# The scan stage of a four-layer kernel: another layout of channels and states on the partitions, transfers in program order, another order of merges, and the gate at PSUM

## The chip, the cores and the metric

The kernel runs on one core of one Trainium2 chip. The metric is device time in microseconds (us) for one execution of the whole program. TensorE, VectorE, ScalarE and GpSimd (POOL) compute, the SP queue issues nearly all transfers, and 16 DMA engines carry them out.

## The reference

Four layers follow each other on four images of 128 channels and 64x64 pixels, all in float32: a spatial attention, two pairs of shift convolution and adder convolution, a gated attention with a small network, and a state-space (Mamba) layer that scans the 4,096 pixels of an image in both directions. The change lies in the last layer alone. What its scan computes, for 256 channels d, 16 states n and 4,096 steps l of each image:

```python
def _selective_scan(u, delta, A, Bm, Cm, Dv, z):
    dA = jnp.exp(jnp.einsum('bdl,dn->lbdn', delta, A))
    dBu = jnp.einsum('bdl,bnl,bdl->lbdn', delta, Bm, u)
    ...
    h = a * h + bu          # at each step, from h0 = 0
    ...
    y = jnp.einsum('lbdn,bnl->bdl', hs, Cm) + Dv[None, :, None] * u
    return y * _silu(z)
...
y = y_f + flip(y_b)         # forward scan, and the scan of the reversed sequence
mamba_out = jnp.einsum('bdl,od->blo', y, out_proj_w)
x_processed = _layer_norm(mamba_out, ln_w, ln_b)
return f_mamba + gamma * f_low
```

## The kernel before

The first three layers and the preparation of the fourth (`layer3_prepare`) leave in DRAM, for each image, the step sizes `delta_d`, the products of step size and input `du_d`, the convolved input `xs_d`, the gate `sz_d` (256 rows of 4,096 each), the rows B and C in `xdbl_d` (16 each), and the low part `low_d`. The function `layer3_scan` does the rest, and only it is changed.

**Tiles.** One tile is 8 channels with their 16 states: 128 partitions, 4,096 steps. There are 4 images x 2 halves of the channels x 16 = 128 tiles. In the kernel before, partition p holds state p // 8 of channel p % 8. Each tile is worked in two halves of 2,048 steps (`h`). For each half a load brings 8 rows of `delta_d` (`dl`) and one brings 8 rows of `du_d` (`du`), each repeated for the 16 states (L933, 1,024 KB each); per image and half there is one load of B and one of C (L924, 1,024 KB), each row repeated for the 8 channels.

**Pieces.** A tile's scan is cut into 8 pieces of 1,024 steps, four forward and four backward, in the order of line 911. For each piece (L944 to L960) ScalarE computes the decay `da` into PSUM (L953) and VectorE scans (L955), each piece starting from the last value of the one before. POOL has made the scan's other input before that, `dbu = du * B` (L941). A piece of each direction covers the same pixels, so TensorE adds the two directions by multiplying both by the identity into one PSUM bank of 512 steps (`merge`, L970), ScalarE copies the bank to SBUF (L979), POOL multiplies 2,048 steps by C (L983), and TensorE sums the 16 states of each channel into 32 rows of the tile `y` (L992). After four tiles `y` holds 32 channels: ScalarE copies it (L1002) and a transfer stores it to `y_d` as 4 blocks of 32 rows by 512 steps (L1004).

**Finish.** For each 512 steps of an image, `finish` loads `y_d`, `xs_d` and `sz_d` (L1014), adds the skip term `2 * D * xs` (L1016, L1017), multiplies by the gate on VectorE (L1018), and does the output projection (L1022), the layer norm (L1024 to L1032) and the sum with `low_d` (L1030, L1033). It runs for one image beside the scan of the next, and for the last image after everything else.

**Order.** A loop over tiles `n` and pieces `e` (L1041 to L1071) writes the operations of several tiles between each other: pieces of tile n, merges of tile n - 1, products by C and sums of tiles n - 1 and n - 2, inputs of tile n + 1. A scheduler then orders the instructions of each engine by their dependencies and by when buffers come free; only what is put in `keep_in_program_order` stays where it is written. In the kernel before, no transfer of the scan stage is: SP issues `dl`, `du` and the loads of `finish` where the scheduler put them. Buffers: `dl` 3, `du` 2, `dbu` 3, `h` 6, `m` 2, B and C 3 each, `y` one for each half.

Of the kernel before, what the change touches and what calls it, by code (L numbers as in the profile page):

```python
# [16 lines left out]
P = 128  # L17
# [821 lines left out]
def layer3_scan(  # L839
# [9 lines left out]
    with ExitStack() as ctx:  # L849
        cp = ctx.enter_context(tc.tile_pool(name="l4c", bufs=1))  # L850
        bc = ctx.enter_context(tc.tile_pool(name="l4bc", bufs=3))
# [6 lines left out]

        of8 = cp.tile([P, ND], F32, name="of8")
        nc.vector.tensor_reduce(of8, cm.ident.rearrange("p (n d) -> p d n", d=ND), AX.X, ALU.add)  # L860
# [5 lines left out]
        for j in range(4):  # L866
            nc.vector.tensor_copy(rows_of[:, j, ND * j : ND * (j + 1)], of8)

        a = []
        for name, src in (("af", a_log), ("ab", ab_log)):  # L870
# [5 lines left out]
            for c in range(2):  # L876
                spread = sb.tile([P, D_STATE, ND], F32, tag="spread", name=f"{name}_s{c}")
                nc.vector.tensor_tensor(
                    spread,
                    t[:, c, :].unsqueeze(2).broadcast_to([P, D_STATE, ND]),  # L880
                    of8.unsqueeze(1).broadcast_to([P, D_STATE, ND]),
                    ALU.mult,
                )
                pa = ps_m.tile([P, P // ND], F32, tag="mg", name=f"{name}_p{c}")
                nc.tensor.matmul(pa, spread.rearrange("p n d -> p (n d)"), group, start=True, stop=True)
                nc.vector.tensor_copy(at[:, c, :], pa)
            a.append(at)

        d2 = cp.tile([P, 2], F32, name="d2")
        nc.sync.dma_start(d2, d_param)  # L890

        nc.vector.tensor_scalar(d2, d2, 2.0, None, ALU.mult)
        skip = cp.tile([P, 2, P], F32, name="skip")
        for c in range(2):
            nc.vector.tensor_scalar(skip[:, c, :], cm.ident, d2[:, c : c + 1], None, ALU.mult)
# [20 lines left out]
        def by_states(b, h):  # L916

            if (b, h) not in by_image:
                got = []
                for what in range(2):  # L920
                    t = bc.tile([P, HL], F32, tag="BC"[what], name=f"{'BC'[what]}{b}_{h}")
                    r = DT_RANK + D_STATE * what
                    src = xdbl_d[b, r : r + D_STATE, halves[h]]
                    nc.sync.dma_start(t, src.unsqueeze(1).broadcast_to([D_STATE, ND, HL]))  # L924
                    got.append(t)
                by_image[b, h] = got
            return by_image[b, h]

        def by_channels(src, n, h, tag, bufs):
# [3 lines left out]
            nc.sync.dma_start(t, rows8.unsqueeze(0).broadcast_to([D_STATE, ND, HL]))  # L933
            return t

        def inputs(n, h):

            b = tiles[n][0]
            du = by_channels(du_d, n, h, "du", 2)
            t = big.tile([P, HL], F32, tag="dbu", bufs=3, name=f"dbu{n}_{h}")  # L940
            nc.gpsimd.tensor_tensor(t, du, by_states(b, h)[0], ALU.mult)  # L941
# [20 lines left out]
        def block_of(e):  # L962
            return (1, e) if e < 4 else (0, e - 4)
# [11 lines left out]
        def copied(n, e):  # L975
            h, k = block_of(e)
            if k == 0:
                st[n, "m", h] = big.tile([P, HL], F32, tag="m", bufs=2, name=f"m{n}_{h}")
            nc.scalar.copy(st[n, "m", h][:, bass.ts(k, BK)], st.pop((n, "mg", e)))  # L979

        def times_c(n, h):
            m = st[n, "m", h]
            nc.gpsimd.tensor_tensor(m, m, by_states(tiles[n][0], h)[1], ALU.mult)  # L983

        def sums(n, h):

            j = tiles[n][2] % 4
# [3 lines left out]
            for g in range(4):  # L991
                nc.tensor.matmul(  # L992
                    st["y", h][32 * g : 32 * g + 32, :], rows_of[:, j, :], m[:, bass.ts(g, BK)],
                    start=(j == 0), stop=(j == 3), skip_group_check=True,
                )

        def evacuate(n, h):
            b, c, i = tiles[n]
            if i % 4 < 3:
                return  # L1000
            t = sb.tile([P, BK], F32, tag="ye", name=f"ye{n}_{h}")
            nc.scalar.copy(t, st.pop(("y", h)))  # L1002
            r = 8 * (i - 3)
            nc.sync.dma_start(y_d[b, c, r : r + 32, halves[h]].rearrange("r (g w) -> g r w", g=4), t)  # L1004

        def finish(b, k):
# [3 lines left out]
            gated = []  # L1010
            for c in range(2):
                yx = sb.tile([P, 3, BK], F32, tag="yx", name=f"yx{v}_{c}")
# [199 lines left out]
```

## Time and profile before

| What | Value |
|---|---|
| median of three runs | 23,432.48 us (23,413.33 to 23,440.21) |
| the profiled execution: time, span | 23,406.72 us, 23,404.9 us |
| first issue of a load of the scan stage (`dl`) | 20,072.2 us |
| first and last scan of L955 begin | 20,088.3 us, 23,291.9 us |
| scans: those that take a value over, and those that start a direction | 768 at 2,349 ns, 256 at 2,290 ns |
| decays of L953 | 1,024 at 1,118 ns |
| copies of L979 | 1,024 at 581 ns |

The page gives the span in 40 equal slices of 585 us; a digit is the busy share of an engine in tenths. The row DMA is the mean busy share of the 16 DMA engines, and GB/s what they moved. A group row gives line, engine and operation, the tiles and shapes, the count, busy us and mean ns of one, and the idle time before it with what ended it. The waits give who waited for whom, the us in total, how many times, and the longest. A table of stretches gives for each stretch of time the busy us of the engines, the granted TensorE clock, the DMA share and the GB/s.

### The profile page before, as it was taken

How to read it: one execution, taken by the hardware profiler on the slowest of the kernel's cores; microseconds unless marked ns; L12 is line 12 of the kernel's file. 1: busy time of each engine (PE TensorE's matmuls, PEld its weight loads, DVE VectorE, ACT ScalarE, POOL GpSimd, SP SyncE). 2: the span in 40 equal slices, each digit the busy share in tenths (PEclk: the TensorE clock that was granted, in tenths of full speed). 3: DMA queues.
4: the chain of work that ended last, by engine and by line, in shares of the span. 5: the costliest groups of instructions: out<-in, count | busy, mean ns of one | idle time of the engine just before them, and what ended most of it. 6: DMA issues, size and time to landing. Idle time of an engine off the chain costs nothing. (4 is left out here: it accounts for less than half of the span.)

```text
span 23404.9 us, 347773 instructions
## 1 busy us (share of the span) xinstructions
PE 21561.9 (92%) x146624; PEld 7793.4 (33%) x146624; DVE 20131.0 (86%) x15018; ACT 19315.0 (83%) x13440; POOL 3763.5 (16%) x1710
## 2 busy tenths in 40 slices
PE   9999999999999999999999999999997557677777
PEld 4443333333333333433333333333333222222222
DVE  7887999999999999989999999999997765777776
ACT  5666999999999999989999999999997224555554
POOL 5662000000000000000000000000000000577776
PEclk9999999999999999999999999999998776899999
DMA  0000000000000000000000000000000002788886
GB/s 13 11 5 12 1 3 7 1 3 5 3 3 1 3 1 3 2 11 3 5 3 1 3 7 1 3 1 3 3 1 32 0 0 99 186 197 190 192 192 170
DMA packets 174502, 809.06 MB, mean 35 GB/s; under 512 B 22716, under 2 KB 23364, under 8 KB 102788
## 3 DMA queue, kind: packets, MB, share of 16 engines
q1 hardware_dynamic: 172356, 778.42, 13.2%
q8 instruction: 1146, 18.78, 0.3%
q10 hardware_dynamic: 576, 8.39, 0.1%
q14 instruction: 424, 3.47, 0.0%
HBM read 658.15 MB, written 128.58 MB: 34 GB/s over the span
## 5 line engine op out<-in xcount | busy, mean ns | idle before, releaser
L396 ACT ACTIVATE a1a<-a1pb,a1wn 128x2048 f32<-128x2048 f32 x4096 | 7792.7, 1995 | 198.7 <-PE a1pa L342 102.0
L396 ACT ACTIVATE a2a<-a2pb,a2wn 128x2048 f32<-128x2048 f32 x4096 | 7791.3, 1996 | 136.8 <-PE a2pa L342 94.8
L407 DVE TENSOR_SCALAR a2d<-a2pb,a2wa 128x2048 f32<-128x2048 f32 x4096 | 4993.8, 1282 | 212.8 <-PE a2pa L342 212.5
L407 DVE TENSOR_SCALAR a1d<-a1pb,a1wa 128x2048 f32<-128x2048 f32 x4096 | 4993.2, 1282 | 207.1 <-PE a1pa L342 206.6
L342 PE MATMUL a2pa<-a2a,a2pick 128*32 128x512 f32 x32768 | 4576.2, 593 | 31.4 <-ACT a2a L396 31.4
L342 PE MATMUL a1pa<-a1a,a1pick 128*32 128x512 f32 x32768 | 4570.0, 593 | 31.3 <-ACT a1a L396 31.3
L342 PE MATMUL a2pa<-a2d,a2pick 128*32 128x512 f32 x32768 | 4436.8, 594 | 46.6 <-DVE a2d L407 46.4
L342 PE MATMUL a1pa<-a1d,a1pick 128*32 128x512 f32 x32768 | 4434.7, 594 | 47.1 <-DVE a1d L407 47.0
L425 DVE SCALAR_TENSOR_TENSOR a1a<-a1pb,a1wa,a1a 128x2048 f32<-128x2048 f32 x1024 | 2406.5, 2350 | 322.5 <-ACT a1a L396 322.5
L425 DVE SCALAR_TENSOR_TENSOR a2a<-a2pb,a2wa,a2a 128x2048 f32<-128x2048 f32 x1024 | 2406.3, 2350 | 314.0 <-ACT a2a L396 314.0
L342 PEld LDWEIGHTS a2pa<-a2a,a2pick 128*32 128x32 f32 x32768 | 1490.7, 110 | 2368.2 <-issue 2045.2
L342 PEld LDWEIGHTS a1pa<-a1a,a1pick 128*32 128x32 f32 x32768 | 1487.4, 110 | 2370.3 <-issue 2030.4
L970 PE MATMUL mg<-h,ident 128*128 128x512 f32 x4096 | 1998.7, 639 | 258.1 <-ACT m L979 211.0
L342 PEld LDWEIGHTS a2pa<-a2d,a2pick 128*32 128x32 f32 x32768 | 1348.3, 109 | 2470.9 <-issue 1921.1
L342 PEld LDWEIGHTS a1pa<-a1d,a1pick 128*32 128x32 f32 x32768 | 1345.1, 109 | 2472.3 <-issue 1902.8
L955 DVE TENSOR_TENSOR_SCAN h<-da,h,dbu 128x1024 f32<-128x1024 f32 x768 | 1804.3, 2349 | 86.2 <-POOL dbu L941 4.4
L970 PEld LDWEIGHTS mg<-h,ident 128*128 128x128 f32 x4096 | 796.8, 203 | 1503.9 <-issue 881.1
L190 POOL TENSOR_TENSOR ssum<-ssum,et 128x512 f32<-128x512 f32 x960 | 1228.9, 1280 | 233.5 <-ACT et L185 166.8
L983 POOL TENSOR_TENSOR m<-m,C 128x2048 f32<-128x2048 f32 x256 | 1157.0, 4519 | 641.7 <-DVE h L955 335.4
L941 POOL TENSOR_TENSOR dbu<-du,B 128x2048 f32<-128x2048 f32 x256 | 1153.3, 4528 | 24.5 <-DMA du<-du_d 19.4
L155 ACT COPY et<-pe 128x512 f32<-128x512 f32 x1024 | 595.5, 582 | 592.1 <-PE pe L153 575.8
L153 PE MATMUL pe<-q,k 128*128 128x512 f32 x2048 | 1051.1, 596 | 8.7 <-DVE mx L163 8.1
(265 smaller groups left out, 13276.7 us busy)
## 6 DMA issues: line engine op xcount, KB each, us to landing
dl<-delta_d SPq DMA_DIRECT2D x256, 1024.0 KB
du<-du_d SPq DMA_DIRECT2D x256, 1024.0 KB
xs_d<-xs SPq DMA_DIRECT2D x8, 2048.0 KB
sz_d<-sz SPq DMA_DIRECT2D x64, 256.0 KB
delta_d<-dv SPq DMA_DIRECT2D x32, 512.0 KB
du_d<-du SPq DMA_DIRECT2D x32, 512.0 KB
y_d<-ye SPq DMA_DIRECT2D x64, 256.0 KB
yx<-xs_d SPq DMA_DIRECT2D x64, 256.0 KB
```

What stands on the lines that cost most here:

```text
L153: nc.tensor.matmul(pe, k[:, bass.ts(j, P)], unit[u, "q"], start=True, stop=True)
L155: nc.scalar.copy(et, pe)
L190: nc.gpsimd.tensor_tensor(unit[u, "sum"], unit[u, "sum"], at, ALU.add)
L342: nc.tensor.matmul(pa[s][32 * g : 32 * g + 32, :], pick[v][:, 31 - jj : 63 - jj], d[:, bass.ts(s, BK)], start=False, stop=False, skip_grou ...
L396: nc.scalar.activation(rows(at), view(t), AF.Abs, bias=wn[t][:, co : co + 1], scale=0.5 if g == q else 1.0,)
L407: nc.vector.tensor_scalar(rows(dt), view(t), wa[:, t, co : co + 1], None, ALU.max)
L425: nc.vector.scalar_tensor_tensor(at, view(MAX_TAP), wa[:, MAX_TAP, co : co + 1], at, ALU.max, ALU.add)
L941: nc.gpsimd.tensor_tensor(t, du, by_states(b, h)[0], ALU.mult)
L955: nc.vector.tensor_tensor_scan(t[:, cols][:, s], da[:, s], st[n, "dbu", h][:, cols][:, s], 0.0 if e % 4 == 0 else st["last"], ALU.mult, AL ...
L970: nc.tensor.matmul(pm, cm.ident, st[n, way, h][:, bass.ts(k, BK)], start=(way == 0), stop=(way == 1))
L983: nc.gpsimd.tensor_tensor(m, m, by_states(tiles[n][0], h)[1], ALU.mult)
```

## The change

- **Layout.** Partition p now holds state p % 16 of channel p // 16. The loads of `dl` and `du` read 8 rows, each 16 times in a row; those of B and C read the 16 rows, 8 times over. The small constant matrices follow (`of16`, `of8`, `spread`).
- **Transfers** of the stage go through `moved`, which pins them in program order on SP. B and C have two buffers each in place of three. `du` is asked for up to two tiles ahead.
- **Merges.** The order of `block_of` changes: a tile's first two merges (`e` of 6 and 7) are written beside the tile's own last backward pieces, the other six beside the next tile. `m` has three buffers.
- **Gate at PSUM.** `xs_d` and `sz_d` are loaded beside the sums of four tiles, as 4 blocks of 32 rows (`blocks_of`); the skip term is four more matmuls into `y` (L1025 of the changed kernel), and VectorE multiplies `y` by the gate straight out of PSUM. What is stored to `y_d` is the gated result. `finish` then loads `y_d` and `low_d` alone.
- **Finish** is a generator that goes one step every second piece; `lb` and `lw` are applied on ScalarE, the product with the scale of the norm on POOL.

The core of the diff:

```diff
-        bc = ctx.enter_context(tc.tile_pool(name="l4bc", bufs=3))
+        bc = ctx.enter_context(tc.tile_pool(name="l4bc", bufs=2))
...
+        def moved(out, src):
+            tc.keep_in_program_order(nc.sync.dma_start(out, src))
...
-                    nc.sync.dma_start(t, src.unsqueeze(1).broadcast_to([D_STATE, ND, HL]))
+                moved(t, src.unsqueeze(0).broadcast_to([ND, D_STATE, HL]))
...
             rows8 = src[b, c, ND * i : ND * (i + 1), halves[h]]
-            nc.sync.dma_start(t, rows8.unsqueeze(0).broadcast_to([D_STATE, ND, HL]))
+            moved(t, rows8.unsqueeze(1).broadcast_to([ND, D_STATE, HL]))
...
         def block_of(e):
-            return (1, e) if e < 4 else (0, e - 4)
+            return (0, e - 2) if 2 <= e < 6 else (1, e - 6 if e > 5 else e + 2)
...
-                st[n, "m", h] = big.tile([P, HL], F32, tag="m", bufs=2, name=f"m{n}_{h}")
+                st[n, "m", h] = big.tile([P, HL], F32, tag="m", bufs=3, name=f"m{n}_{h}")
...
+        def blocks_of(t, n, h):
+            b, c, i = tiles[n]
+            r = 32 * (i // 4)
+            return t[b, c, r : r + 32, halves[h]].rearrange("r (g w) -> g r w", g=4)
+
+        def beside_sums(n, h):
+            if tiles[n][2] % 4 == 0:
+                for name, src in (("xs", xs_d), ("sz", sz_d)):
+                    t = sb.tile([P, BK], F32, tag=name, bufs=2, name=f"{name}4_{n}_{h}")
+                    moved(t, blocks_of(src, n, h))
+                    st[name, h] = t
...
-                    start=(j == 0), stop=(j == 3), skip_group_check=True,
+                    start=(j == 0), stop=False, skip_group_check=True,
                 )
-        def evacuate(n, h):
-            ...
-            nc.scalar.copy(t, st.pop(("y", h)))
-            r = 8 * (i - 3)
-            nc.sync.dma_start(y_d[b, c, r : r + 32, halves[h]].rearrange("r (g w) -> g r w", g=4), t)
+            if j == 3:
+                for g in range(4):
+                    rows32 = slice(32 * g, 32 * g + 32)
+                    nc.tensor.matmul(
+                        st["y", h][rows32, :], skip[rows32, c, q, :], st["xs", h][rows32, :],
+                        start=False, stop=True, skip_group_check=True, tile_position=(32 * g, 32 * g),
+                    )
+        def gate(n, h):
+            if tiles[n][2] % 4 == 3:
+                t = st.pop(("sz", h))
+                nc.vector.tensor_tensor(t, st.pop(("y", h)), t, ALU.mult)
+                st["gated", h] = t
+        def store(n, h):
+            if tiles[n][2] % 4 == 3:
+                moved(blocks_of(y_d, n, h), st.pop(("gated", h)))
...
         def finish(b, k):
...
-                yx = sb.tile([P, 3, BK], F32, tag="yx", name=f"yx{v}_{c}")
-                for q, src in enumerate((y_d, xs_d, sz_d)):
-                    nc.sync.dma_start(yx[:, q, :], src[b, c, :, ck])
-                py = ps_m.tile([P, BK], F32, tag="mg", name=f"py{v}_{c}")
-                nc.tensor.matmul(py, cm.ident, yx[:, 0, :], start=True, stop=False)
-                nc.tensor.matmul(py, skip[:, c, :], yx[:, 1, :], start=False, stop=True)
-                nc.vector.tensor_tensor(yx[:, 0, :], py, yx[:, 2, :], ALU.mult)
+                moved(gated[:, c, :], y_d[b, c, :, ck])
+            moved(fl, low_d[b, :, ck])
+            yield
...
+            nc.scalar.activation(fl, fl, AF.Identity, bias=lb)
...
+            nc.scalar.activation(mo, po, AF.Identity, scale=lw)
             nc.scalar.activation(sq, po, AF.Square)
...
-            nc.vector.scalar_tensor_tensor(rs, po, lw, rs, ALU.mult, ALU.mult)
-            nc.gpsimd.tensor_scalar(rs, rs, lb, None, ALU.add)
-            nc.gpsimd.tensor_tensor(fl, rs, fl, ALU.add)
-            nc.sync.dma_start(out[b, :, ck], fl)
+            nc.gpsimd.tensor_tensor(mo, mo, rs, ALU.mult)
+            yield
+            nc.gpsimd.tensor_tensor(fl, mo, fl, ALU.add)
...
+            moved(out[b, :, ck], fl)
...
+                k = n if e > 5 else n - 1
+                if in_range(k):
+                    merge(k, e)
+                k, was = (n, e - 1) if e > 6 else (n - 1, (e - 1) % 8)
+                if in_range(k):
+                    copied(k, was)
+                if e == 0:
+                    delta(n + 1, 0)
+                    ...
+                    if in_range(n - 2):
+                        beside_sums(n - 2, 0)
+                if e == 1:
+                    if n > 0:
+                        products_in(n + 1, 1)
+                    ...
+                if e == 2:
+                    times_c(n - 1, 1); sums(n - 2, 0)
+                if e == 3:
+                    inputs(n + 1, 0); gate(n - 2, 0)
+                if e == 4:
+                    store(n - 2, 0); beside_sums(n - 1, 1)
+                if e == 5:
+                    inputs(n + 1, 1); sums(n - 1, 1)
+                if e == 6:
+                    delta(n + 1, 1)
+                    products_in(n + 2, 0)
+                    gate(n - 1, 1)
+                if e == 7:
+                    times_c(n - 1, 0); store(n - 1, 1)
+                if e % 2 == 0:
+                    next(steps, None)
```

(In the last part the tests for the range of tiles are left out and calls are joined in a line; `delta` and `products_in` issue the loads of `dl` and `du` through `by_channels`.)

## The prediction

> **What bounds the kernel now.** I read the page's 40 slices first, to see where the change acts: only in the last seven slices (from 20,072 us on) does the DMA row leave zero. This is the scan stage.
>
> ```profile
> DVE  7887999999999999989999999999997765777776
> POOL 5662000000000000000000000000000000577776
> DMA  0000000000000000000000000000000002788886
> GB/s 13 11 5 12 1 3 7 1 3 5 3 3 1 3 1 3 2 11 3 5 3 1 3 7 1 3 1 3 3 1 32 0 0 99 186 197 190 192 192 170
> ```
>
> No engine is full there, yet the 16 DMA engines are busy 0.8 of the time. Then the costliest groups, for the stage's floors (count, busy us, mean ns, idle before):
>
> ```profile
> L955 DVE TENSOR_TENSOR_SCAN h<-da,h,dbu 128x1024 f32<-128x1024 f32 x768 | 1804.3, 2349 | 86.2 <-POOL dbu L941 4.4
> L983 POOL TENSOR_TENSOR m<-m,C 128x2048 f32<-128x2048 f32 x256 | 1157.0, 4519 | 641.7 <-DVE h L955 335.4
> L941 POOL TENSOR_TENSOR dbu<-du,B 128x2048 f32<-128x2048 f32 x256 | 1153.3, 4528 | 24.5 <-DMA du<-du_d 19.4
> ```
>
> With the 256 scans that start a tile (586.2 us), VectorE has 2,390 us of scans; POOL has 2,310 us. The stage takes 3,200 us. So there are some 800 us that no engine's work explains. The waits say why: VectorE waits for merges (L970) that free its `h` buffers, POOL for scans.
>
> ```profile
> DVE h L955 <- PE mg L970: 504.4, 252, 4.9
> POOL m L983 <- DVE h L955: 335.4, 56, 6.5
> POOL dbu L941 <- DMA du<-du_d: 19.4, 2, 14.7
> ```
>
> Loads are hardly ever waited for (19.4 us). That is the state to be lost or kept: a loop of scan, merge, copy and multiplication paces the stage, and loads arrive just in time. How near they are to being the bound is in a table of stretches, where the last two columns are the busy share of 16 DMA engines and GB/s:
>
> ```profile
> 17949.00:17975.00 26.00, 2.07 (x2) 0.50 (x2) 17.77 (x8) 9.01 (x5) 0.42 (x4) 0.50 1.00 415
> 19926.00:19954.00 28.00, 14.47 (x33) 5.91 (x32) 19.32 (x11) 10.55 (x20) 0.00 (x0) 0.85 0.98 222
> 21009.00:21012.00 3.00, 3.00 (x9) 1.22 (x8) 2.90 (x2) 1.63 (x2) 3.00 (x1) 1.00 1.01 218
> 23311.00:23315.00 4.00, 1.53 (x4) 0.38 (x2) 0.69 (x1) 0.43 (x1) 3.43 (x1) 1.00 0.24 62
> 20090.00:23290.00 3200.00, 2523.27 (x6410) 897.59 (x6411) 2426.18 (x1095) 1754.83 (x2169) 2347.30 (x556) 0.91 0.81 192
> ```
>
> First row: plain loads of whole images, 16 engines busy, 415 GB/s, so 25.9 per engine. Second: six B and C loads (16 rows, each to 8 partitions) back to back: 222/(16 x 0.98) = 14.2 per engine. Third: `dl` and `du` (8 rows, the set repeated 16 times): 13.5. Broadcast loads run at half the plain rate, whichever rows they read. Fourth: one y_d store alone, whose DRAM side is written as 4 blocks of 32 rows: share 0.24, so 3.9 of 16 engines, at 62/3.84 = 16.1 each. Last: the stage, 0.81.
>
> **The change, part by part.** All sums are against the profiled execution (23,406.7 us; 23,404.9 of them are its span). The median of the runs shown is 26 us (0.1%) above it.
>
> *Merges earlier, deeper prefetch, gate at PSUM.* The 504 us wait on L970 should go: half of the merges of a tile now begin while its last backward pieces run, and `du` is asked for a tile ahead. VectorE keeps its 1,024 scans and 64 gates (0.67 us each, L1018's row), and loses 32 operations of L1031 (0.75 us). TensorE loses 256 of L1016 and L1017 (0.6 us) and gains 512 narrow ones for the skip term (bounded by 0 and 0.7 us, L992's row: at most 360 us, beside a TensorE that is 0.79 busy now and would have far more room). ScalarE swaps 64 evictions (0.58 us) for 64 Identity operations. None of these is a bound. Alone, they could bring the stage from 3,200 us to the VectorE floor of about 2,430 us, that is 0 to 770 us of gain. They give it only if the loads keep up; what is late next is the loads.
>
> *The layout, and the number of DMA engines.* `dl` and `du` are now written as 8 rows, each repeated 16 times; before, it was 16 repeats of 8 rows. B and C become 8 repeats of 16 rows. So the outermost count of the source falls from 16 to 8 in all 528 large loads. The fourth row above is the only look that this trace gives at an outermost count under 16 in a large transfer: a count of 4 went to 4 engines, although its SBUF side has 128 partitions. I take it that a count of 8 goes to 8.
>
> [...]
>
> The rate of each of the 8 engines is not in the trace. Ends: 13.5 (they are slowed as the 16 are now) and 25.9 (plain loads). I take 13.9, the mean of the two broadcast rows, since these are the nearest, and since B and C (16 distinct rows) and `dl` (8 rows) run alike, so that the slowing hardly comes from many engines reading one row. The side written to remains as a cause, and it is written in the same 128 partitions as before.
>
> [...]
>
> Large loads: 512 + 16 at 1.049 MB are 553.6 MB; at 8 x 13.9 = 111 GB/s, 4,988 us (at 207 GB/s, 2,674).
>
> *Four-engine transfers.* `xs` and `sz` are now loaded as 4 blocks of 32 rows: 128 loads of 0.262 MB, where the kernel before used plain 128-row loads. With the 64 y_d stores (kept, later pinned behind other transfers) that is 50.3 MB at 4 x 16.1 GB/s: 781 us; at 25.9 per engine, 486. I put them on engines that the large loads use too, which the trace doesn't tell; if they lie elsewhere, these 781 us are hidden.
>
> *Sixteen-engine transfers.* 64 loads of gated rows, 32 `fl`, 32 `out`: 33.6 MB, at 16.1 to 25.9 per engine some 100 us.
>
> The sum on the busiest engines is 4,988 + 781 + 100 = 5,869 us, or 46 us a tile, against 19 us of VectorE per tile: the compute parts all hide behind it.
>
> *Is the queue ever empty?* The SP queue issues in program order, each load when its buffer is free. The latest is the second `dl` of the next tile, which waits for the sixth decay (L953) of this one; behind it stand two `du`, one `dl` and the stores. When loads are the bound, that decay comes about 4 pieces (10 us) after the preceding second `dl` has landed, while three more loads (28 us) are still in the queue. So pinning costs nothing while loads bind, and the DMA engines stay busy. (If loads did not bind, a store that waits for its gate would hold up the loads behind it by at most a piece or two, 2 to 5 us per half of four tiles, 320 us at the most.)
>
> *Ends.* Setup gains a dozen operations of 0.15 to 0.3 us (L878, L901), under 5 us. The stage begins with the first `dl` issue at 20,072 us. After the last large load there remain six pieces (15 us) and the tail: now 115 us from 23,290 on, about 20 us less without the skip matmuls and L1031, of which 25 us are transfers already in the sum: 85 us.
>
> Total: 20,072 + 5,869 + 85 = 26,026 us span. I say **26,000 us**, 11% slower.
>
> **Rivals.**
> 1. *Fewer engines, but some of them faster* (0.15). The extra transfers shift engines against each other, so that the slowing of neighbours ends for some, or the four-engine transfers lie on other engines. Then the rest bound: 20,072 + 4,988 + 100 + 85 = 25,245; I give it 24,900 to 25,500. Against: in the 28 us of back-to-back loads the rate stayed at 14.2.
> 2. *The 215 to 222 GB/s is one limit for all, not a limit per engine* (0.12). Then 8 engines reach 207: 2,674 + (486 to 781) + 100 + 85, so 23,420 to 23,710. Against: nothing but the equal rates of B, C and `dl`; the trace has no broadcast on fewer engines that would tell.
> 3. *The outermost count doesn't set the engines* (0.08). All large loads stay at 218 GB/s: 2,539 us, and with `xs`, `sz` on 16 engines too some 450 more. The earlier merges then show, as loads are issued earlier: 20,072 + 2,990 + 85 = 23,150, 1.1% faster. It decides from the point where loads land within the 25 us that a tile takes now. Against: the store's 0.24.
> 4. *Loads bind and are also held up* (0.03): over 26,690, where loads wait for stores and decays as well.
>
> **How the numbers follow.** The forecast has 0.62; its own range goes from rates of 14.2 with 25.9 for the small transfers (4,873 + 486 + 81 + 85: 25,600) to 13.5, with the 128 small loads at half of 16.1 as the broadcast loads are at half the plain rate (5,126 + 1,043 + 261 for the stores + 100 + 85: 26,690). The 80% range takes in rival 1: 24,900 to 26,690. Runs here tell 0.2% (47 us) from no change. Faster: rival 3 (0.08). Same: a part of rival 2 (0.04). Slower: the rest, 0.88.
>
> **What would show it.** In the scan stage of the changed kernel: DMA share about 0.5 where it was 0.81, and 105 to 115 GB/s where it was 192; ScalarE's decays waiting for `dl`, POOL's products for `du`, in thousands of us; the scan rows still 2,349 ns, VectorE's tenths at 4; the 504 us wait on merges gone. A share of 0.8 with 190 GB/s or more would refute the engine count (rival 3); a share near 0.5 with some 200 GB/s would refute the rate (rival 2).

## The result, and the profile after

The changed kernel takes 24,487.65 us (24,472.36 to 24,511.94), the one before 23,427.26 us beside it: a ratio of 1.0454, 95% interval 1.0436 to 1.0472. The forecast was 26,000 us, 24,900 to 26,690. The direction is right, but the time lies 412 us below the range. The rest of this document looks for the 1,500 us that the forecast has too many.

The page of the changed kernel, the same rows of the 40 slices (612 us each) as shown of before:

```profile
DVE  7887999999999999899999999999976655555554
POOL 5661000000000000000000000000000015555554
DMA  0000000000000000000000000000000034444443
GB/s 15 8 5 11 1 6 3 1 3 6 1 3 1 3 3 1 12 1 6 3 1 3 6 1 3 1 3 3 1 31 0 36 119 143 146 152 154 146 156 119
```

The scan stage is the last seven or eight slices again. The DMA row fell from 8 to 4, as predicted. But the GB/s row says 143 to 156, not 105 to 115: half the engines, each faster than forecast. The costliest groups of the same page (count | busy us, mean ns | idle before, and what ended most of it):

```profile
L965 DVE TENSOR_TENSOR_SCAN h<-da,h,dbu 128x1024 f32<-128x1024 f32 x768 | 1804.4, 2350 | 1337.5 <-ACT da L963 1228.5
L963 ACT ACTIVATE da<-dl,af 128x1024 f32<-128x1024 f32 x512 | 565.6, 1114 | 1589.7 <-DMA dl<-delta_d 1377.8
L951 POOL TENSOR_TENSOR dbu<-du,B 128x2048 f32<-128x2048 f32 x256 | 1156.2, 4516 | 1678.4 <-DMA du<-du_d 1475.4
```

The durations are those of before (2,350, 1,114 and 4,516 ns). What changed is the idle time in front of them: VectorE waits for the decay, the decay for `dl`, POOL for `du`. The waits of the stage say the same, with the wait on merges still there:

```profile
POOL dbu L951 <- DMA du<-du_d: 1475.4, 196, 23.6
ACT da L963 <- DMA dl<-delta_d: 1377.8, 153, 23.7
...
DVE h L965 <- PE mg L980: 420.3, 166, 12.0
```

And the stretch from the first scans to near the end (PE, PEld, DVE, ACT, POOL busy, then granted clock, DMA share, GB/s):

```profile
20090.00:24300.00 4210.00, 2608.41 (x6686) 903.59 (x6687) 2403.26 (x1080) 1723.28 (x2144) 2334.62 (x554) 0.82 0.48 149
```

A DMA share of 0.48 at 149 GB/s is 149/(16 x 0.48) = 19.4 GB/s for each engine that is busy, where the forecast had 13.9 for the large loads. The trace's packet records give it more directly. A packet of a large load is 8,192 bytes. In before it takes 568 ns in the mean (median 607), in the changed kernel 411 (median 321): 19.9 GB/s per engine. The number of engines is as forecast. Behind its issue, the semaphore of a large load is updated 8 times in place of 16, that of a transfer in 4 blocks 4 times; for 70% of the time exactly 8 engines are busy, and for some 2% none.

So the theory after the result: **eight engines carry the large loads, and what was mis-sized is the rate of each**. Two questions are left. Why do they run at 19.9 when 16 run at 14? And does the rest of the change cost or bring anything beside them?

### The profile page after: what moved, and what is told of

Read it like the earlier page. It is cut to its first block, busy times and chain, and to the rows that moved or that the text cites. A ratio compares the mean times of both kernels' runs of the same rounds, so it can differ in the third digit from the quotient of the medians.

```text
span 24479.9 us, 348201 instructions
## 1 busy us (share of the span) xinstructions
PE 21647.0 (88%) x146880; PEld 7794.3 (32%) x146880; DVE 20098.0 (82%) x14994; ACT 19303.0 (79%) x13441; POOL 3756.3 (15%) x1710
## 4 chain that ended last, share of the span: by engine, by line
PE 74%; DMA 11%; DVE 7%; ACT 3%; issue 3%; POOL 1%; SPq 1%; DVEq 0%; ACTq 0%; POOLq 0%
PE a1pa L342 29%; PE a2pa L342 29%; DMA dl<-delta_d 8%; PE pe L153 4%; PE pav L196 3%; DVE h L965 2%; DMA du<-du_d 2%; DVE g L658 1%; PE a1pc L323 1%; PE a2pc L323 1%; PE mg L980 1%; PE pd L643 1%; ACT da L963 1%; ACT a2a L396 1%; PE a2pa L352 1%
## 5 line engine op out<-in xcount | busy, mean ns | idle before, releaser
L980 PE MATMUL mg<-h,ident 128*128 128x512 f32 x4096 | 2217.6, 687 | 1503.8 <-ACT m L989 1367.4
L965 DVE TENSOR_TENSOR_SCAN h<-da,h,dbu 128x1024 f32<-128x1024 f32 x768 | 1804.4, 2350 | 1337.5 <-ACT da L963 1228.5
L963 ACT ACTIVATE da<-dl,af 128x1024 f32<-128x1024 f32 x512 | 565.6, 1114 | 1589.7 <-DMA dl<-delta_d 1377.8
L951 POOL TENSOR_TENSOR dbu<-du,B 128x2048 f32<-128x2048 f32 x256 | 1156.2, 4516 | 1678.4 <-DMA du<-du_d 1475.4
```

Source lines behind the costliest of these rows:

```text
L951: nc.gpsimd.tensor_tensor(t, du, by_states(b, 0, h), ALU.mult)
L963: nc.scalar.activation(da, st[n, "delta", h][:, cols], AF.Exp, scale=a[way][:, c, i : i + 1])
L965: nc.vector.tensor_tensor_scan(t[:, cols][:, s], da[:, s], st[n, "dbu", h][:, cols][:, s], 0.0 if e % 4 == 0 else st["last"], ALU.mult, AL ...
L980: nc.tensor.matmul(pm, cm.ident, st[n, way, h][:, bass.ts(k, BK)], start=(way == 0), stop=(way == 1))
```

## The experiments

All times are medians of 4 to 10 runs beside runs of the kernel before on the same chip (23,416 to 23,427 us). The runs of e2 spread from 23,741 to 23,890 us and those of e3 from 24,620 to 24,806 us; the others lie closer together.

### What the layout is worth (e1, e2)

Run e1 is the changed kernel with the layout of before:

```diff
-                moved(t, src.unsqueeze(0).broadcast_to([ND, D_STATE, HL]))
+                moved(t, src.unsqueeze(1).broadcast_to([D_STATE, ND, HL]))
...
-            moved(t, rows8.unsqueeze(1).broadcast_to([ND, D_STATE, HL]))
+            moved(t, rows8.unsqueeze(0).broadcast_to([D_STATE, ND, HL]))
```

(with `of8` in `rows_of` and `spread` turned to match). Run e2 is the reverse: the kernel before with the new layout alone.

> The changed kernel, with the partitions laid out as before (state outermost), so that the large loads again read 16 repeats of 8 rows, and B and C 16 rows 8 times. Theory A (the outermost count sets the number of DMA engines, and the loads bind): the large loads go over 16 engines; at the 14 GB/s per engine that broadcast loads had in the kernel before they take some 2,490 us, with some 870 us of small transfers on four engines and 90 us of others, so 20,072 + 3,450 + 85 = 23,610 us, or down to 22,900 if engines run at the 20 GB/s that they have in the changed kernel. DMA share 0.7 or more in the scan stage. Theory B (the pinned order: stores that wait for the gate hold up the loads behind them, 975 us of SP waits): stays within 200 us of 24,488.

> The kernel before, with only the layout changed (channel outermost). Theory A: 8 engines for the large loads: 3,480 us at the 20 GB/s per engine of the changed kernel, 270 us of stores on four engines, 200 us of others, so 20,072 + 3,950 + 110 = 24,130 us; at 14 GB/s per engine 25,600. DMA share about 0.5. Theory B: within 100 us of 23,427, since nothing is pinned.

e1 took 23,761.76 us (ratio 1.0145, 1.013 to 1.016), e2 23,847.14 us (1.0174, 1.0149 to 1.02). Theory A has the direction and the DMA share of both, but e1 lies 150 us above its longest time and e2 283 us below its shortest. Stretches of e1 and then of e2:

```profile
20090.00:23290.00 3200.00, 2298.16 (x6113) 799.67 (x6114) 2199.20 (x989) 1584.22 (x1966) 2143.11 (x508) 0.88 0.80 180
```

```profile
20090.00:23290.00 3200.00, 2233.60 (x5609) 780.21 (x5610) 2132.06 (x966) 1528.89 (x1900) 2061.90 (x487) 0.87 0.52 170
```

The share moves between 0.8 and 0.5 with the layout and with nothing else: in these four kernels an outermost count of 16 goes with 16 engines (0.81 before, 0.80 in e1), one of 8 with 8 (0.48 in the changed kernel, 0.52 in e2). The layout costs 726 us in the changed kernel and 426 us in the kernel before. Two things were not expected. In e2 the eight engines reach 170/(16 x 0.52) = 20.4 GB/s each, with a third of the four-engine transfers of the changed kernel (64 stores). And e1, which has 16 engines and the new order of merges, is still 340 us slower than before.

### Why the eight engines run faster than forecast (e3, e4, e8, e9)

Run e3 takes away the four-engine transfers of the changed kernel: `xs`, `sz` and `y_d` go in four transfers of 32 rows each, meant for 16 engines (the records of before show 16 landings for transfers of 64 and of 128 rows; for 32 rows I have no count).

```diff
+        def in_blocks(out, src):
+            for g in range(4):
+                part = slice(32 * g, 32 * g + 32)
+                if len(out.shape) == 2:
+                    moved(out[part, :], src[g])
+                else:
+                    moved(out[g], src[part, :])
...
-                    moved(t, blocks_of(src, n, h))
+                    in_blocks(t, blocks_of(src, n, h))
...
-                moved(blocks_of(y_d, n, h), st.pop(("gated", h)))
+                in_blocks(blocks_of(y_d, n, h), st.pop(("gated", h)))
```

> The changed kernel, with each load of xs and sz blocks and each store of gated blocks cut into four transfers of 32 rows, whose outermost count is 32, so that they use 16 engines. Theory A: the four engines that had 870 us more than the other four lose it; the eight then have 3,480 + 200 us: 20,072 + 3,680 + 85 = 23,840 us. If the small transfers on four engines were what set engines out of step, and so gave 20 GB/s per engine where the kernel before had 14, the large loads slow to 4,990 us: 25,340 us. Theory B: little change, since the stores wait for the gate as before: 24,400 to 24,500.

It took 24,729.89 us (1.0542, 1.0514 to 1.0571): 242 us more than the changed kernel, although it was to free four of the eight engines of some 800 us of work. That lies between the two times of theory A (23,840 and 25,340).

```profile
20090.00:23290.00 3200.00, 1909.27 (x4570) 656.19 (x4570) 1641.22 (x740) 1187.64 (x1463) 1599.24 (x376) 0.78 0.52 135
```

At the same number of engines the rate fell from 149 to 135 GB/s, and a packet of a large load now takes 499 ns (median 513) in place of 411 (median 321). So beside the four-engine transfers the large loads ran faster. But that is only about half of the difference: the forecast's 13.9 GB/s would be 589 ns for a packet, and 499 are reached without any such transfer. (e3 also has four times as many small transfers in the queue, so its time shows less than its packets do.) Run e4 has loads alone, with no computation.

> Leaves out all of the computation and does only loads, stage by stage, each stage back to back: plain 128 rows; 16 repeats of 8 rows; 8 rows 16 times each; 16 rows 8 times each; 4 rows 8 times each (32 partitions); 4 rows 16 times each (64 partitions); 8 rows 8 times each (64 partitions); blocks of 32 rows; and a mix of the third with blocks. Theory A1 (a rate per engine of some 14 GB/s for all broadcast loads): the third has half the rate of the second, 111 against 222 GB/s; four engines have 55 GB/s whether they write 32 or 64 partitions. Theory A2 (engines share a side written to, and get out of step by the blocks): the third is at 111 alone and higher in the mix; four engines that write 32 partitions reach 104 GB/s (26 each), four that write 64 partitions 55. Theory A3 (one limit of some 220 GB/s for all broadcast loads): the third is near 207 GB/s alone, and the four-engine stages both at 104.

Its GB/s slices (48 us each):

```profile
GB/s 401 266 220 220 221 221 114 110 110 110 110 110 110 110 111 146 238 237 237 237 108 106 91 106 107 106 106 106 138 209 168 102 107 111 123 151 175 189 161 118
```

From the left: plain rows at 401; 16 engines x 8 partitions at 220; 8 engines x 16 partitions, the loads of the changed kernel, at 110. That is 13.8 GB/s per engine: **alone, these loads have just the rate that the forecast took**. Next come 16 engines for B and C (238); 4 engines on 32 and on 64 partitions (106); 8 engines on 64 partitions (209, so 26 for each, where the plain rows have 25); four-engine blocks (102 to 107). The last slices are eight large loads and two four-engine blocks in turn: the rate climbs from 107 to 189. Theory A2 had this and the 110; it missed the four engines on 64 partitions (106 in place of 55). Run e8 varied the number of partitions for each engine and in all. How the partitions of a load are spread over its engines is assumed in it; the records don't name the engine of a packet.

> Loads alone, no computation (the output is not the reference's), in stages that differ in how many partitions lie between what two engines write at the same time; a load of r rows with the outermost count k gives each of k engines r partitions in a row. Earlier runs: 16 engines x 8 partitions 220 GB/s, 8 x 16 110, but 8 x 8 and 4 x 16 (64 partitions in all) at full 26 per engine. Theory A: what slows is that one engine writes partition p while another writes p + 64, which happens when 64 is a multiple of r and 128 partitions are written. Then 16 x 6 (96 partitions), 16 x 7 and the pair of 16 x 6 with 16 x 2 to the last 32 partitions run at 380 to 415 GB/s, 8 x 14 at 205 to 210, 4 x 32 at 54, 4 x 24 at 104 to 107, 2 x 32 (64 partitions) at 52. Theory B: what slows is that any loads over more than 64 partitions from repeated rows share one limit of 220 GB/s (13.9 per engine): 16 x 6 and 16 x 7 at 220, 8 x 14 at 110, 4 x 32 and 4 x 24 at 54. [...]

Stretches, the last column GB/s: 16 engines x 8, 16 x 7, 8 x 14, 4 x 32, 2 x 32.

```profile
20.00:110.00 90.00, 0.00 (x0) 0.00 (x0) 1.00 1.01 225
...
290.00:420.00 130.00, 0.00 (x0) 0.00 (x0) 1.00 1.01 287
...
720.00:900.00 180.00, 0.00 (x0) 0.00 (x0) 1.00 0.51 206
950.00:1160.00 210.00, 0.00 (x0) 0.00 (x0) 1.00 0.25 106
...
1370.00:1590.00 220.00, 0.00 (x0) 0.00 (x0) 1.00 0.13 53
```

8 x 14 runs at 206 where 8 x 16 ran at 110, so the partitions matter and theory B falls. But theory A falls too: 16 x 7 reached 287, not 380, and 4 x 32 reached 106, not 54. The packet records give a hint why. In the fastest stretches a packet takes 309 ns. In the 2 x 32 stage the first ones take 905, 880, 309, 309, 631, 626, 339, 352, 628, 639 ns; soon nearly all take 309 (96% of the whole stage at most 318). My guess, from these times alone: two engines slow each other while they write in step (some 630 ns are about twice 309), and here they fall out of step by themselves. No run shows the step itself. Run e9 tries the guess, in its second stage with one extra transfer of outermost count 8, for eight engines alone:

```python
stage("halves", [halves64] * 40)                                    # 16 engines x 4, twice a load
stage("lag", [halves64] * 4 + [apart(8, 4, HL)] + [halves64] * 40)  # one transfer on 8 engines between
stage("o16x8", [outer(16, 8)] * 16 + [blocks] * 2 + [outer(16, 8)] * 24)
stage("i8x16", [inner(8, 16)] * 16 + [blocks] * 2 + [inner(8, 16)] * 32)
```

> Loads alone, no computation (the output is not the reference's). [...] Four stages, the queue never drained within one. (1) 40 loads cut into two transfers of 64 partitions each, 16 engines x 4 partitions; (2) the same, with one transfer for engines 0 to 7 alone (4 packets each) after the fourth load, so that these lag by half a load; (3) 16 loads of 16 engines x 8 partitions, two transfers of blocks on 4 engines, 24 more loads; (4) 16 loads of 8 engines x 16 partitions, two transfers of blocks, 32 more loads. [...] Theory B (the extra transfers don't matter; the rates in the kernels come from computation beside them): (1) and (2) alike at 220 to 250, (3) 220 and (4) 110 throughout.

Stretches of it: the first stage, the second behind its extra transfer, the third behind its blocks, the fourth before its blocks and some 100 us behind them.

```profile
20.00:180.00 160.00, 0.00 (x0) 0.00 (x0) 1.00 1.02 229
220.00:300.00 80.00, 0.00 (x0) 0.00 (x0) 1.00 1.01 383
430.00:490.00 60.00, 0.00 (x0) 0.00 (x0) 1.00 1.01 230
520.00:650.00 130.00, 0.00 (x0) 0.00 (x0) 1.00 0.51 112
780.00:860.00 80.00, 0.00 (x0) 0.00 (x0) 1.00 0.50 208
```

The first two rows are the same loads. One transfer of 0.26 MB between them took the rate from 229 to 383 GB/s for as long as the queue had work. In the fourth stage two block transfers on four engines took 112 to 208, and the median packet from 619 to 309 ns. So theory B, with the first two stages alike and the fourth at 110 throughout, falls. Without such a transfer the loads of the fourth stage stayed at 110 GB/s for 430 us (e4). So this much is shown: **a transfer that only some of the engines take part in took the loads behind it from 229 to 383 GB/s and from 112 to 208**; that it shifts engines against each other fits the guess, but isn't shown. It isn't always at once: in the second stage the rate jumped, in the fourth it stayed at 108 to 132 GB/s for some 100 us behind the blocks. Nor is it always so: with 16 engines x 8 partitions, in the third row, nothing is gained (230). Why isn't shown.

The changed kernel issues 192 such transfers itself. In a kernel, e2 shows the change of rate best. Its first four-engine store was issued at 20,299 us, the second at 20,331 us; a stretch before and one behind them:

```profile
20100.00:20299.00 199.00, 84.37 (x183) 29.40 (x184) 93.06 (x40) 62.71 (x74) 80.80 (x18) 0.69 0.51 113
20375.00:20775.00 400.00, 305.76 (x816) 110.43 (x816) 317.98 (x137) 226.48 (x280) 304.82 (x68) 0.93 0.51 189
```

From 113 to 189 GB/s with the same engines: the mean packet fell from 590 to 352 ns. (Two plain loads on 16 engines were issued right behind the second store, so the stores aren't the only candidates.) In the same second stretch e3, without four-engine transfers, is at 137 GB/s. Yet its packets too fall to 320 ns and less for some 25 us at a time and come back to 560 and more. What starts that in e3 stays open, and with it half of the rate that the forecast missed.

### What the rest of the change costs (e5, e6, e7, e11)

> The changed kernel with two parts undone: the layout (as before, 16 engines for the large loads) and the four-engine transfers of xs, sz and y_d (cut into four transfers of 32 rows each, on 16 engines). With the layout alone undone it took 23,762 us, some 340 us more than the kernel before, though the 504 us merge wait was gone. Theory A: those 340 us and more come from the 192 four-engine transfers, which keep 4 of 16 engines busy for some 870 us while the large loads need all 16. Then 553.6 MB of large loads at 220 GB/s (2,516 us) and 84 MB of others at up to 400 (210 us) bind: 20,072 + 2,730 + 85, so 22,900, up to 23,200. Theory B: they come from the pinned order; stores stand in the SP queue until their gate is done (946 us of such waits with the layout undone), with the next loads behind them. Cutting the transfers leaves that order as it is: 23,600 to 23,800.

> The changed kernel with the layout as before and without the pinning of transfers (the scheduler orders them), the four-engine transfers kept. Theory A (four-engine transfers): still 23,650 to 23,800. Theory B (stores that wait in the queue for their gate): 22,950 to 23,300, and SP's waits for the gate are gone.

> The changed kernel with its new layout, the transfers of the scan stage not pinned. Theory A (the eight engines of the large loads bind, the queue hardly empties): 24,400 to 24,600, no more than 0.4% from the changed kernel. Theory B (the pinned order holds loads up also here, 975 us of SP's waits for the gate): several hundred us less, 23,900 to 24,200.

> The changed kernel with the old layout, the small transfers on 16 engines, and the transfers not pinned. With either of the last two the old layout took 23,350 to 23,410 us, with neither 23,762. Theory A (the two costs are one: a pinned store on 4 engines holds up the loads behind it; then the 16-engine rate binds): no more to gain, 23,300 to 23,410. Theory B (two separate costs that add up): 23,000 to 23,060.

The edit that unpins is one line:

```diff
         def moved(out, src):
-            tc.keep_in_program_order(nc.sync.dma_start(out, src))
+            nc.sync.dma_start(out, src)
```

| Run | layout | small transfers | order on SP | us | ratio to before (interval) |
|---|---|---|---|---|---|
| changed | new | 4 engines | pinned | 24,487.65 | 1.0454 (1.0436 to 1.0472) |
| e7 | new | 4 engines | free | 24,229.1 | 1.0362 (1.0336 to 1.0389) |
| e3 | new | 32 rows each | pinned | 24,729.89 | 1.0542 (1.0514 to 1.0571) |
| e1 | old | 4 engines | pinned | 23,761.76 | 1.0145 (1.013 to 1.016) |
| e6 | old | 4 engines | free | 23,350.28 | 0.9971 (0.996 to 0.9982) |
| e5 | old | 32 rows each | pinned | 23,406.3 | 0.9994 (0.9985 to 1.0003) |
| e11 | old | 32 rows each | free | 23,312.22 | 0.9953 (0.9937 to 0.9969) |

e5 lies between the two theories' times. e6 lies 50 us above the range of the theory of the pinned order (B), and SP's waits for the gate shrink but aren't gone. e7 lies 29 us above that theory's range, and e11 fits its theory A. With the old layout the four-engine transfers cost 356 us while pinned and 38 us while free. Pinning costs 412 us with them and 94 us without. So the two costs are mostly one, as theory A of e11 had it: a pinned transfer that waits stands in front of the next loads. The layout, which cost 726 and 426 us above, costs 879 us between e6 and e7 and 1,324 us between e5 and e3: its price depends on what else is in the queue. The waits of the SP queue show it: the changed kernel, then e1, then e6.

```profile
SPq L927 <- DVE sz L1033: 909.5, 62, 22.7
```

```profile
SPq L927 <- DVE sz L1033: 804.4, 56, 19.3
```

```profile
SPq L927 <- DVE sz L1033: 159.7, 60, 12.5
```

SP stands 804 to 910 us in front of stores whose gate (L1033) isn't done, and 160 us when the order is free. In e1 exactly four engines are busy for 11% of the stage and none for 9%. With the new layout a free order gains 259 us.

### What the merges bring (e12)

Run e12 is the kernel before with the new order of merges alone: `block_of` of the changed kernel, merges of `e` 6 and 7 beside the tile's own pieces, `m` with three buffers, B and C with two so that they fit, and the products by C and the sums moved to where their merges are done.

```diff
-            return (1, e) if e < 4 else (0, e - 4)
+            return (0, e - 2) if 2 <= e < 6 else (1, e - 6 if e > 5 else e + 2)
...
-                if 0 < n <= last + 1:
-                    merge(n - 1, e)
+                k = n if e > 5 else n - 1
+                if 0 <= k <= last:
+                    merge(k, e)
```

> The kernel before with the new order of merges alone (order of blocks, two merges beside a tile's own last backward pieces, three buffers for m, two for B and C so that they fit; layout, transfers, gate and finish as before). Theory A (the merges come earlier, but the loads at some 220 GB/s bind close behind): DMA share up from 0.81 to 0.85 or more, the 504 us wait on merges down, waits for du and dl up, 23,200 to 23,400. Theory B (the new order doesn't help even where loads allow it, since the loop of scan, merge, copy and product paces as before): DMA share 0.81, 23,400 or more.

It took **23,045.96 us (0.984, 0.9826 to 0.9855): 375 us faster than before, and the fastest of all runs here**. Theory A is right on the merges and on the DMA share, and the gain is larger than it expected. A stretch, and three rows of the waits:

```profile
20090.00:23000.00 2910.00, 2443.82 (x6525) 840.83 (x6526) 2445.01 (x1105) 1753.43 (x2191) 2373.72 (x564) 0.97 0.89 214
```

```profile
DVE h L955 <- PE mg L970: 164.3, 246, 4.1
...
ACT da L953 <- DMA dl<-delta_d: 35.1, 12, 5.0
...
POOL dbu L941 <- DMA du<-du_d: 27.4, 5, 15.3
```

The wait of VectorE on merges fell from 504 to 164 us, the DMA share rose from 0.81 to 0.89 at 214 GB/s. The loads run at the rate that 16 engines had before (565 ns for a packet, 568 before) and leave the DMA engines empty for 5% of the stage, but they are hardly waited for: 35 and 27 us. VectorE is busy for 2,445 of the 2,910 us. So that the loads bind close behind, as theory A has it, isn't shown.

Between e12 and e11 lie the gate at PSUM, the new `finish`, the deeper prefetch of `du`, and the small transfers: e11 has 768 of 32 rows each, e12 64 stores on four engines and 128 plain loads. e11 takes 266 us more. VectorE's waits in e11:

```profile
DVE h L965 <- PE mg L980: 322.8, 54, 11.6
DVE h L965 <- POOL dbu L951: 256.8, 46, 13.5
```

They are 164 and 26 us in e12. All waits of VectorE together are 702 us in e11 and 421 in e12, which is about the whole difference. A packet of a large load takes 588 ns in e11 and 565 in e12, and the DMA engines stand empty for 8% of e11's stage and 5% of e12's, but POOL and ScalarE wait for loads for only 90 and 10 us in e11. So the 266 us show in the order of merges, copies and products more than in the loads. I didn't separate the gate, the new `finish`, the prefetch and the cut transfers.

### Loads over 230 GB/s (e10, e13, e14, e15)

The 383 GB/s of e9 suggest a faster kernel: each large load cut into two transfers of 64 partitions, 16 engines x 4 partitions.

```diff
-            moved(t, rows8.unsqueeze(1).broadcast_to([ND, D_STATE, HL]))
+            for a in range(2):
+                rows4 = rows8[4 * a : 4 * a + 4]
+                moved(t[64 * a : 64 * a + 64, :], rows4.unsqueeze(0).broadcast_to([D_STATE, 4, HL]))
```

> The changed kernel with its small transfers on 16 engines (32 rows each) and with another layout: the first four channels of a tile on partitions 0 to 63, the other four on 64 to 127, each large load cut into two transfers of 16 engines x 4 partitions. Theory A (engines that fall out of step run at full rate; each load now has a time at which two halves of the engines may write different halves of the partitions): loads at 250 to 400 GB/s, and then the merges' new order shows: 22,600 to 23,100. Theory B (they stay in step, 220 GB/s): as with both parts undone, 23,350 to 23,500.

> The kernel of run e10 (64 partitions to a transfer, small transfers on 16 engines), not pinned. In e10 the DMA engines stood empty 30% of the stage and the time was 24,251. Theory A (e10 lost this to the pinned order: twice as many transfers in one queue, each waiting for its buffer): 23,300 to 23,450, as the unpinned kernel with the old layout (23,312), bound by 228 GB/s. Theory B (it lost it in the order in which the engines' own instructions were put): 23,900 or more, with the DMA engines empty again for a fifth of the time or more.

> As e13, with one more transfer a tile: 8 rows of delta_d x 512 columns, 16 times, to a tile that nothing reads, on engines 0 to 7 alone (16 packets of 2 KB, estimated 16 x 84 ns = 1.3 us, about half of a half load), so that these engines lag behind the others. With loads alone such a lag took the rate from 228 to 385 GB/s. Theory A (loads bind in e13, and a lag lasts while the queue has work): stretches over 300 GB/s in the stage, 100 to 400 us less than e13. Theory B (the queue runs empty so often that the engines fall back into step, or loads do not bind): within 50 us of e13.

> The kernel of run e12 (before, with the new order of merges alone, 23,046 us) with each large load cut into two transfers of 64 partitions (16 engines x 4 partitions), as in e13. [...] Theory A (the 64-partition transfers are no slower, and the engines' order was to blame in e13): 22,700 to 23,050, with stretches over 230 GB/s. Theory B (cutting the loads in two makes the scheduler put the engines' instructions in an order that leaves them waiting, whatever the rest): 23,800 or more, with the DMA engines empty for a fifth of the time or more.

None is faster than before: e10 24,251.05 us (1.0355, 1.0336 to 1.0373), e13 24,169.39 (1.032, 1.0305 to 1.0336), e14 24,400.38 (1.0418, 1.0401 to 1.0436), e15 24,633.51 (1.0519, 1.0501 to 1.0537). e10 and e14 fit neither of their theories, e13 and e15 theory B. e13's stretch, and e15's with two of its waits:

```profile
20090.00:23000.00 2910.00, 1971.14 (x4880) 685.09 (x4880) 1740.62 (x784) 1267.30 (x1554) 1700.25 (x402) 0.81 0.66 155
```

```profile
20090.00:23000.00 2910.00, 1836.01 (x4174) 644.93 (x4174) 1584.21 (x711) 1148.08 (x1416) 1536.47 (x360) 0.76 0.58 137
```

```profile
POOL m L991 <- ACT m L987: 1403.9, 227, 13.9
DVE h L963 <- POOL dbu L949: 1306.9, 122, 21.3
```

The DMA engines stand empty for 30% of the stage in e13 and 39% in e15, so these loads don't bind. In e15 VectorE waits for POOL's `dbu`, and POOL stands in front of products by C whose copies aren't done. e15 differs from e12 only in the cut loads and the layout that they need, and in it the order of the instructions on ScalarE and POOL differs through the whole stage. It is likely that the scheduler, with twice the transfers to place, chose an order in which engines wait for each other; I did not show it by fixing e12's order. With e14's added transfers the large loads' packets took 487 ns in place of 568, and e14 took 231 us more than e13: loads were not what bound. (To make room, e14 also has three buffers in place of four in the layer norm; what each of the two cost isn't shown.) So the kernel that uses 383 GB/s was not found.

## Why the prediction was wrong, point by point

- **The direction, the place and the number of engines: right.** "I take it that a count of 8 goes to 8": share 0.48, eight landings a load (and four for a transfer in 4 blocks), and 0.8 again in e1 with the layout undone.
- **The rate of each engine: the step that failed.** The prediction says "I take 13.9, the mean of the two broadcast rows", and so 111 GB/s and 4,988 us for 553.6 MB. For these loads alone that is right (110 GB/s in e4, 112 in e9). In the kernel it is 8 x 19.9 = 159 GB/s and 3,476 us: 1,512 us too many. The two rows were taken from stretches in which only such loads ran, and the changed kernel mixes them with transfers on four engines. Without these a packet takes 499 ns (e3), with them 411, where 13.9 GB/s would be 589: they explain about half of the 1,512 us, and the cause of the other half stays open. The trace of before couldn't show the effect: there 64 four-engine stores ran beside the loads on 16 engines, whose packets still took 568 ns.
- **Rival 1 named the extra transfers** ("the extra transfers shift engines against each other") and got 0.15, on the ground that in 28 us of back-to-back loads the rate stayed at 14.2. That stretch has no four-engine transfer in it, so it could not speak against the rival. The runs show the gain (112 to 208 GB/s in e9), not the shift. Its price, 24,900 to 25,500, was also too high: it left 4,988 us for the engines that stay slow, and in fact more than half of the packets took under 340 ns (median 321).
- **The four-engine transfers: 781 us forecast, some 800 us measured.** Right in size: in the first 1,000 us of the stage, where no other transfer has packets of 2 KB, these take 129 to 136 ns, and each of the four engines has 6,144. (The 870 us in the expectations is too high by this.) They run on engines that the large loads use, as assumed: 12 engines are busy at once for only 0.1% of the time. What the sum didn't hold is that the loads run faster beside them: 411 ns for a packet, and 499 in e3 without them, which is 242 us slower.
- **"So pinning costs nothing while loads bind": wrong, 259 us (e7).** The step followed the loads in the queue and not the stores. SP stands 910 us in front of stores whose gate isn't done, and the engines move 149 GB/s in the stage where e7 has 156. The bracket behind that step ("320 us at the most" if loads did not bind) has about the right size for e7, and is too low for the old layout, where pinning costs 412 us.
- **The tail, from the landing of the last large load: 85 us forecast, 166 us measured.** In e7, with a free order, it is 97, so most of the difference comes with the pinning.
- **The sum.** With the measured terms, and the forecast's 100, it reads 20,072 + 3,476 + 800 + 100 + 166 = 24,614, which is some 130 us over the measured span. Probably the four-engine transfers are not wholly in the way of the loads; no run shows it.
- **"The 504 us wait on L970 should go": it is 420 us in the changed kernel**, since VectorE now mostly waits for loads and the merges still run late after them. The reason given for it was misread as well: two of a tile's eight merges begin beside its last backward pieces, not half. Alone, in e12, it falls to 164 us, and the gain of 375 us lies within the 0 to 770 that were named.
- **The gate and `finish`: "None of these is a bound" missed a cost.** With the layout of before and a free order (e11), they, the prefetch and the small transfers in 768 parts cost 266 us beside e12.

The whole difference, 1,067 us against the runs of before beside e12, taken apart by steps (each from the run before it): merges -375 (e12), gate, `finish`, prefetch and cut small transfers +266 (e11), pinning +94 (e5), four-engine transfers while pinned +356 (e1), layout +726. With another order of these steps the shares would differ: the layout alone is worth 426 to 1,324 us, depending on the run that it is added to.

## What to carry to other kernels

Look at the outermost count of both sides of every large transfer before changing a layout: here a change from 16 to 8 on the side read left 8 of the 16 engines at work (DMA share 0.81 to 0.48) and cost 426 to 1,324 us of 23,400, and a store written as 4 blocks had 4 (share 0.24 before). A rate read from a stretch of uniform transfers is not the rate in a mixture: here transfers on a few engines nearly doubled that of the loads behind them (112 to 208 GB/s in e9), or held up a whole pinned queue (356 us). When several edits come in one change, try them singly; here one of them alone was worth -1.6% and was buried under the others.

## What was not expected of the hardware

- One transfer of 0.26 MB on 8 of 16 engines raised the rate of the following loads from 229 to 383 GB/s, and this lasted until the stage ended and the queue ran empty, some 100 us. A packet of 8 KB takes 309 ns in the fast stretches and some 610 to 630 ns in the slow ones.
- Some loads become fast by themselves within a load or two (2 x 32 and 4 x 32 partitions in e8, 96% of the packets at most 318 ns), others don't while alone (8 x 16 partitions for 430 us, 16 x 8 for some 200 us, both in e4). What decides this stays open.
- TensorE's granted clock in the scan stage differs between the runs: 0.97 in e12 (busy 0.84 of the stage), 0.91 before (0.79), 0.82 in the changed kernel (0.62), 0.76 in e15 (0.63). The same 4,096 merge matmuls took 621 ns in the mean in e12 and 710 in e15. No run changes the clock alone.
